# Two-layer graph network on one Trainium2 core: attention slots taken in pairs, scores in quarter tiles, and part of the norm work moved to ScalarE and GpSimd

## The chip, the core and the metric

The kernel runs on one of the eight cores of a Trainium2 chip. The metric is the device time of one execution in microseconds (us), and lower is better. The engines are named as in the profile: PE is the matrix engine (PEld is its weight loading), DVE the vector engine, ACT the scalar engine, POOL GpSimd, and SP the engine that only issues transfers. Each engine works through its own instructions in order and waits on semaphores for the others.

## What is computed

Eight graphs (`B = 8`) of 2048 nodes with 256 features pass through two layers that share one adjacency matrix. All data is float32.

```python
# layer 0: attention with a softmax in each chunk of 256 neighbours, 4 heads of 64
q, k, v = x @ Wq.T + bq, x @ Wk.T + bk, x @ Wv.T + bv
scores = clip(q . k / sqrt(64), -10, 10);  scores = where(mask == 0, -10, scores)
attn = softmax(scores over the 256 nodes of a chunk)
ctx = sum over the 8 chunks of attn @ v
out = layernorm(ctx @ Wo.T + bo + x) * gamma + beta
x = layernorm(x + out)
# layer 1: additive attention, 4 heads of 64
Wh = x @ W;  e = leaky_relu(s_src[i] + s_dst[j], 0.2), masked to -inf
x = layernorm(x + elu(softmax_j(e) @ Wh))
```

## The kernel before

**Slots.** Layer 0 of one graph (a "batch" `b`) is cut into 64 slots (`SLOTS`): four groups `q` of 512 query nodes, two head pairs `hp`, and eight chunks `c` of 256 neighbours. A slot has two units `u`, each of 128 neighbours by 512 queries for two heads. For a unit, `scores` (L390) issues two score matmuls, one per head, with 64 rows of contraction each, into a PSUM buffer of two banks (`ps`). DVE evicts it, clipping it against the mask slab (L401, PSUM to SBUF, `pr`). ACT takes the exponential in place (L413). `product` (L427) multiplies the probabilities of one head of the slot with the values; a column of ones in `vaug` yields the softmax sums. It runs twice per slot, `product(s, 0)` and `product(s, 1)`, into one PSUM bank `psC` each time, and ACT copies it out (L434, `raw`). One slot later `normalize` takes the reciprocal of the sums on DVE (L442) and lets POOL multiply and add into the context (L449, L451).

**Layer 1 of the batch before runs along.** While batch `b` is in layer 0, `Layer1` (`lower`) computes layer 1 of batch `b - 1`. `make` (L743) forms a 128 x 1024 tile `e` on DVE from two SBUF inputs, a row and an edge mask; `use` (L765) multiplies it with the node values in 32 matmul passes. A slot takes two tiles (`STEP = 2`). Two tiles are made ahead, and the pool of `e` has three buffers. `close` divides the sums and applies the ELU when a unit of 16 tiles is done.

**Between the layers.** `Between` handles a group of 512 nodes when its context is complete: output projection (`output`, L543), the two norms, and layer 1's projection (`values`, L585). Its steps are hung into the slots of the next group by tables (`BESIDE`, `BEHIND`, `WIDE_...`, `LATER_...`); the number is the slot within the group of 16. `Norm.stats` uses DVE's batch-norm instructions (L492, L495), and POOL forms the factors (L502, L503). The row additions `bias`, `shift`, `scale`, `again` are on DVE (L527, L531, L560, L563). `Close` ends layer 1: it adds layer 0's result (L830, DVE), norms it and stores it; the table `CLOSING` hangs it into the first slots of a batch.

**Order.** All engines are scheduled by hand: an instruction stands on its engine where the Python line issues it. In a slot with layer 1 along, PE does: scores of the next slot, product 0, two `e` tiles, product 1. DVE does: reciprocal, two evictions, the steps of `Between`, two `e` tiles. Batch 0 has no layer 1 beside it and turns the adjacency into masks instead (`Masks.step`, L251 to L255). Between two batches stands a stretch without slots that projects the next batch's queries, keys and values (L334, L350) and finishes the last group. After batch 7, layer 1 of batch 7 runs alone.

**PSUM.** Eight banks: `psA`, two buffers of two banks, for scores and projections; `psC`, one bank, for products; `psL`, two banks, for layer 1's sums; `psM`, one spare bank.

```python
            if s:
                normalize(s - 1)
            if s + 1 < SLOTS:
                scores(s + 1)
            ...
            product(s, 0)
            if s + 1 < SLOTS:
                for u in range(KT):
                    exps(s + 1, u)
            if lower:
                if b + 1 < B or s < SLOTS - LATE:
                    lower.step()
            ...
                product(s, 1)
```

## Time and profile before

| | |
|---|---|
| median of 3 runs | 3752.97 us (3752.59 to 3754.87) |
| the profiled execution | 3753.24 us, span 3751.5 us |
| granted clock of PE over the span | 0.993 |
| PE, DVE, ACT, POOL busy | 97%, 84%, 53%, 36% |
| HBM traffic | 103 GB/s over the span |

The chain of waits shows when the first score matmul of a batch starts, and cuts the span into stages:

| stage | us |
|---|---|
| start, to the first scores | about 61 |
| batch 0, first scores to last scores | 305 |
| batches 1 to 6, first scores to last scores, each | about 384 |
| stretch between two batches (to the next first scores) | 63 to 68 |
| batch 7, first scores to last scores | about 362 |
| layer 1 of batch 7 alone, and the end | 275.5 |

In the profile a line such as `L401 DVE ... pr<-ps,slab 128x1024 ... x1024 | 1194.3, 1207 | 199.2 <-PE ps L390` gives the line of the kernel, the engine, the tiles out and in, the count, busy time in us, the mean of one in ns, and the idle time of the engine just before. PE's matmuls are pipelined: the ends are modelled, so the distance between starts is the safer measure, and the chain of waits gives it as one duration per run of equal instructions. A float32 matmul shows as two passes on PE, so a score matmul counts twice.

### The profile page before, as it was taken

Reading aid. Unit: us, or ns where it says so; the run is one execution under the profiler, and the core shown is the slowest. Engines: PE = TensorE matmul, PEld = TensorE weight load, DVE = VectorE, ACT = ScalarE, POOL = GpSimd, SP = SyncE. Lnnn points to the kernel's source line nnn. Section 1 sums busy time; section 2 is a strip of 40 time slices with the busy share of each in tenths; the row PEclk is TensorE's granted clock in tenths of the full one; section 3 lists DMA queues with packets and bytes.
Section 4 is the critical chain, followed back from the end, with each engine's and each line's share of the span. In section 5 each row is a group of like instructions: output and inputs, shape, how many; then the busy total and the mean of one; then the engine's idle time right before and its main releaser. Section 6 shows DMA issues by size and latency. Waiting matters only on the chain.

```text
span 3751.5 us, 161119 instructions
## 1 busy us (share of the span) xinstructions
PE 3637.1 (97%) x72844; PEld 2699.4 (72%) x72844; DVE 3139.9 (84%) x4213; ACT 1978.7 (53%) x3571; POOL 1366.8 (36%) x1202
## 2 busy tenths in 40 slices
PE   9999999999999999999999999999999999999787
PEld 5656677776777777776777767777677777776676
DVE  5877489986999689995999959998699977997899
ACT  4666455555555555554555545555455555555322
POOL 1445234333433334333443324433334333334300
PEclk9999999999999999999999999999999999999899
DMA  6653334333333333333433334333433333332354
GB/s 163 152 119 70 79 98 110 103 78 113 105 108 106 86 116 107 105 95 88 132 94 103 98 91 136 109 99 81 113 107 108 105 81 113 116 96 76 103 149 137
DMA packets 672098, 398.56 MB, mean 106 GB/s; under 512 B 427312, under 2 KB 591536, under 8 KB 671408
## 3 DMA queue, kind: packets, MB, share of 16 engines
q1 hardware_dynamic: 621408, 354.55, 36.1%
q10 hardware_dynamic: 50000, 33.70, 2.8%
q8 instruction: 570, 9.34, 1.0%
q14 instruction: 120, 0.98, 0.1%
HBM read 331.22 MB, written 56.89 MB: 103 GB/s over the span
## 4 chain that ended last, share of the span: by engine, by line
PE 84%; DVE 7%; issue 3%; ACT 3%; DMA 1%; SPq 1%; ACTq 0%; POOL 0%; DVEq 0%; POOLq 0%
PE pc L427 25%; PE ps L390 23%; PE pa L765 22%; PE pp L334 5%; PE pw L585 3%; PE po L543 3%; DVE e L743 2%; PE pv L350 2%; DVE pr L401 2%; ACT y L507 1%; ACT pr L413 1%; SPq L284 1%; DMA xp<-in_x_dram 0%; DVE y L563 0%; DVE y L560 0%
## 5 line engine op out<-in xcount | busy, mean ns | idle before, releaser
L401 DVE SCALAR_TENSOR_TENSOR pr<-ps,slab 128x1024 f32<-128x1024 f32 x1024 | 1194.3, 1207 | 199.2 <-PE ps L390 195.2
L427 PEld LDWEIGHTS pc<-vaug,pr 128*64 128x64 f32 x32768 | 1038.6, 138 | 405.4 <-issue 299.0
L743 DVE SCALAR_TENSOR_TENSOR e<-srow,gd,et 128x1024 f32<-128x1024 f32 x1024 | 1278.1, 1292 | 14.9 <-DMA srow<-rowD 8.2
L427 PE MATMUL pc<-vaug,pr 128*64 128x65 f32 x32768 | 1153.4, 224 | 15.7 <-ACT pr L413 9.6
L765 PE MATMUL pa<-waug,e 128*64 128x65 f32 x32768 | 1068.9, 224 | 47.9 <-DVE e L743 43.3
L765 PEld LDWEIGHTS pa<-waug,e 128*64 128x64 f32 x32768 | 1015.5, 139 | 65.7 <-DVE e L743 55.9
L413 ACT ACTIVATE pr<-pr 128x1024 f32<-128x1024 f32 x1024 | 1040.3, 1055 | 40.1 <-DVE pr L401 31.1
L390 PE MATMUL ps<-qT,kT 64*128 64x512 f32 x4096 | 1023.8, 616 | 3.9 <-DVE pr L401 3.2
L434 ACT COPY raw<-pc 128x260 f32<-128x260 f32 x1024 | 380.4, 372 | 1194.1 <-PE pc L427 1175.1
L449 POOL TENSOR_TENSOR part<-raw,rd 128x512 f32<-128x512 f32 x448 | 468.0, 1045 | 1375.7 <-DVE rd L442 1361.3
L451 POOL TENSOR_TENSOR acc<-acc,part 128x512 f32<-128x512 f32 x448 | 574.8, 1283 | 35.2
L390 PEld LDWEIGHTS ps<-qT,kT 64*128 64x128 f32 x4096 | 347.0, 185 | 325.7 <-issue 200.8
L442 DVE RECIPROCAL rd<-raw 128x8 f32<-128x8 f32 x512 | 101.4, 198 | 120.4 <-ACT raw L434 119.3
L449 POOL TENSOR_TENSOR acc<-raw,rd 128x512 f32<-128x512 f32 x64 | 66.8, 1043 | 341.4 <-DVE rd L442 341.4
L797 ACT ACTIVATE sums<-sums,dn 128x64 f32<-128x64 f32 x504 | 131.9, 337 | 13.6 <-DVE dn L791 13.6
L502 POOL TENSOR_TENSOR rs_c<-rs_c,nhalf 128x4 f32<-128x4 f32 x32 | 52.7, 1646 | 233.8 <-DVE off_c L501 233.8
L585 PE MATMUL pw<-w_sb,x1T 128*64 128x264 f32 (+1 forms) x856 | 125.4, 392 | 5.7 <-DVE x1T L296 5.7
L334 PE MATMUL pp<-xT,wk_sb 128*128 128x512 f32 x256 | 119.3, 610 | 7.9 <-ACT qT L342 6.6
L543 PE MATMUL po<-wo_sb,qT 128*64 128x256 f32 (+1 forms) x912 | 120.9, 380 | 6.2 <-DVE qT L469 3.4
L334 PE MATMUL pp<-xT,wq_sb 128*128 128x512 f32 x256 | 116.2, 596 | 0.0
L350 PE MATMUL pv<-wv_sb,xT 128*128 128x256 f32 x512 | 115.9, 379 | 0.0
L296 DVE STREAM_TRANSPOSE xT<-xp 128x1024 f32<-128x1024 f32 x28 | 34.8, 1244 | 92.0 <-PE pw L585 77.8
(103 smaller groups left out, 1869.6 us busy)
## 6 DMA issues: line engine op xcount, KB each, us to landing
et<-edgeD SPq DMA_DIRECT2D x512, 256.0 KB, 3.1
slab<-clipD SPq DMA_DIRECT2D x512, 128.0 KB, 3.1
srow<-rowD SPq DMA_DIRECT2D x64, 512.0 KB, 5.1
xg<-in_x_dram SPq DMA_DIRECT2D x32, 512.0 KB, 5.2
x1D<-y ACTq DMA_DIRECT2D x32, 512.0 KB, 3.9
x1g<-x1D SPq DMA_DIRECT2D x32, 512.0 KB, 5.7
out_dram<-o SPq DMA_DIRECT2D x30, 512.0 KB, 3.6
ctxD<-acc ACTq DMA_DIRECT2D x56, 256.0 KB, 2.6
```

The costliest lines, as they stand in the source:

```text
L334: nc.tensor.matmul(pps[c], lhsT=w[:, kc, c * P : (c + 1) * P], rhs=st["xT"][:, kc, :], start=(kc == 0), stop=(kc == KC - 1),)
L390: nc.tensor.matmul(ps[:, k, :], lhsT=kT[rows, hp, t * P : (t + 1) * P], rhs=qT[rows, hp, cols], start=True, stop=True,)
L401: nc.vector.scalar_tensor_tensor(pr, pss[u], -CLIP, slab[:, u, :].unsqueeze(1).to_broadcast([P, 2, CH]), op0=ALU.max, op1=ALU.min,)
L413: nc.scalar.activation(pr, pr, AF.Exp, scale=0.125)
L427: nc.tensor.matmul(pc[z * D : (z + 1) * D, i, :], lhsT=probs[s][u][:, k, i * P + z * D : i * P + (z + 1) * D], rhs=vaug[:, KT * c + u, 2 * ...
L434: nc.scalar.copy(raws[s][:, k], pc)
L449: nc.gpsimd.tensor_mul(part, raw[:, :, :, :D], rd.to_broadcast([P, 2, QT, D]))
L451: nc.gpsimd.tensor_add(accv, accv, part)
L543: nc.tensor.matmul(po[z, k, :], lhsT=qT[:, c, t * P + z.start : t * P + z.stop], rhs=wo_sb[:, c, :], start=(c == 0), stop=(c == KC - 1),)
L585: nc.tensor.matmul(pw[z, k, : F + 2 * H], lhsT=self.x1T[:, c, u * P + z.start : u * P + z.stop], rhs=w1_sb[:, c, :], start=(c == 0), stop= ...
L743: nc.vector.scalar_tensor_tensor(e[:, :w], self.rows[n][:, :w], self.gd[:, h, j : j + 1], self.edge[k // JG][:, j % JG, :w], op0=ALU.max, ...
L765: nc.tensor.matmul(self.pa[i // QT][z * D : (z + 1) * D, i % QT, :], lhsT=e[:, i * P + z * D : i * P + (z + 1) * D], rhs=self.waug[:, j, h ...
```

## The change

- Two slots form a pair, 32 per batch (`PAIRS`; 8 per group, `QP`). `burst(p)` issues the scores of the four units of the next pair one behind the other. Only three PSUM buffers exist for them, so the fourth unit comes after the first unit's eviction. The other three evictions are spread over the pair.
- `unit` computes a unit's scores as four matmuls of 64 x 64 weights ("quarters"), one per head and half of the neighbours, in place of two of 64 x 128.
- PSUM: `psA` becomes three buffers of two banks in rotation, for scores, products, outputs and projections; `psC` and `psM` are gone. `product(s)` does both heads of a slot at once and is copied out in one go.
- The order on PE in a pair: burst of the next pair, two `e` tiles, product of the first slot, two `e` tiles, product of the second slot.
- Norm statistics in the slots move from DVE to ACT (`sums`, `squares`, with an accumulated output) with small POOL steps (`centre`, `factors`). `bias`, `shift`, `scale` of the groups in the slots and `Close.add` of batches 2 to 7 move from DVE to POOL. The stretches between batches and the end keep them on DVE.
- The steps of `Between` stand in new tables by pair, and the second norm of a group ends one group later (`NEXT_...`) or in the stretch between batches (`early`). Buffers: 7 for `pr` (from 4), 2 slabs of double size (from 4), one `y` (from 2).

```diff
+    def unit(s, u):
+        q, hp, c = where[s]
+        t = KT * c + u
         cols = slice(q * CH, (q + 1) * CH)
-        pss = []
-        for u in range(KT):
-            t = KT * c + u
-            ps = two_banks([P, 2, CH], "ps")
+        ps = two_banks([P, 2, CH], "ps")
+        for z in range(2):
             for k in range(2):
                 rows = slice(k * D, (k + 1) * D)
                 nc.tensor.matmul(
-                    ps[:, k, :],
-                    lhsT=kT[rows, hp, t * P : (t + 1) * P],
+                    ps[z * D : (z + 1) * D, k, :],
+                    lhsT=kT[rows, hp, t * P + z * D : t * P + (z + 1) * D],
                     rhs=qT[rows, hp, cols],
...
+    def burst(p):
+        us = units_of(p)
+        pss = [unit(*us[k]) for k in range(3)]
+        evict(*us[0], pss[0])
+        pss.append(unit(*us[3]))
+        return list(zip(us, pss))[1:]
...
+        def sums(self, ks):
+            for k in ks:
+                junk = small.tile([P, F], BF16, tag="junk", name="junk", bufs=1)
+                nc.scalar.activation(
+                    junk, self.src[:, k, :], AF.Copy, accum_out=self.mv[:, k, 0:1]
+                )
+        def centre(self):
+            self.mean = small.tile([P, QT], F32, tag="mean", name="mean_" + self.name)
+            nc.gpsimd.tensor_scalar(self.mean, self.mv[:, :, 0], -1.0 / F, None, ALU.mult)
+        def squares(self, ks):
+            for k in ks:
+                junk = small.tile([P, F], BF16, tag="junk", name="junk", bufs=1)
+                nc.scalar.activation(junk, self.src[:, k, :], AF.Square,
+                    bias=self.mean[:, k : k + 1], accum_out=self.mv[:, k, 1:2])
+        def factors(self):
...
+            nc.gpsimd.tensor_tensor(self.rs, self.rs, nhalf, ALU.pow)
+            nc.gpsimd.tensor_mul(self.off, self.mean, self.rs)
...
+    FIRST_PAIRS = {2: lambda o: o.add((0, 1)), 3: lambda o: o.add((2, 3))}
+    ON_ACT = {2: lambda o: o.a.sums((0, 1)), 3: lambda o: o.a.sums((2, 3)),
+        4: lambda o: o.a.squares((0, 1, 2, 3)), 5: lambda o: o.a.apply(o.y),
+        7: lambda o: o.b2.sums((0, 1, 2, 3))}
+    LATE_ON = {1: lambda o: o.bias(nc.gpsimd),
+        3: lambda o: (o.a.centre(), o.shift(nc.gpsimd)), 4: lambda o: o.a.factors(),
+        5: lambda o: o.scale(nc.gpsimd), 6: lambda o: o.again(), 7: lambda o: o.b2.centre()}
+    LAST_ON_PE = {1: lambda o: o.output((0, 1)), 2: lambda o: o.output((2, 3))}
+    NEXT_FIRST = {2: lambda o: o.load()}
+    NEXT_ON_ACT = {0: lambda o: o.b2.squares((0, 1, 2, 3)), 1: lambda o: o.finish()}
+    NEXT_LATE = {0: lambda o: o.b2.factors(), 3: lambda o: o.turn()}
+    NEXT_LAST = {4: lambda o: o.values((0, 1)), 5: lambda o: o.values((2, 3))}
...
+            if p:
+                normalize(s0 - 1)
+            hook(FIRST_PAIRS, NEXT_FIRST)
+            if more:
+                waiting = burst(p + 1)
+                evict(*waiting[0][0], waiting[0][1])
+                exps(*us[0])
+                exps(*us[1])
+            hook(ON_ACT, NEXT_ON_ACT)
...
+            if along:
+                along.rest(1)
+                along.make()
+            if more:
+                evict(*waiting[1][0], waiting[1][1])
+                exps(*us[2])
+            if along:
+                along.use()
+                along.make()
+                along.use()
+                along.make()
...
+            product(s0)
+            if more:
+                evict(*waiting[2][0], waiting[2][1])
+                exps(*us[3])
+            normalize(s0)
+            if along:
+                along.rest(1)
+                along.use()
+                along.make()
+                along.use()
...
+            hook(LATE_ON, NEXT_LATE)
+            if closing:
+                closing.do(p, "add", "centre", "factors")
...
+            product(s1)
+            hook(LAST_ON_PE, NEXT_LAST)
...
+            table.setdefault(i, []).append((g, "add", nc.gpsimd))
+            table.setdefault(i + 1, []).extend([(g, "sums"), (g, "centre")])
+            table.setdefault(i + 2, []).extend([(g, "squares"), (g, "factors")])
+            table.setdefault(i + 3, []).append((g, "finish"))
...
+    CLOSING = closing_of((0, 1, 3, 5), ((-1, HOME), (0, HOME), (2, HOME_Y), (4, HOME)))
```

In this excerpt the tables are written on fewer lines than in the file. `turn_context` (a DVE transpose, L469) stands in pairs 1 and 6 of a group, ahead of `LATE_ON`.

436 lines of the change are left out of this document (218 added, 218 removed).

## The prediction

> **What bounds the kernel now.** I read the page's busy shares and chain first, then the chain of waits within batch 3, then single groups, then the timeline where DVE and POOL meet.
>
> ```profile
> PE 3637.1 (97%) x72844; PEld 2699.4 (72%) x72844; DVE 3139.9 (84%) x4213; ACT 1978.7 (53%) x3571; POOL 1366.8 (36%) x1202
> PE 84%; DVE 7%; issue 3%; ACT 3%; DMA 1%; SPq 1%; ACTq 0%; POOL 0%; DVEq 0%; POOLq 0%
> ```
>
> PE carries 84% of the chain. The chain of waits inside a batch shows one slot and, in the stretch between batches, a plain projection:
>
> ```profile
> 1947.16 1.92 PE ps L390 x8
> 1949.08 1.08 PE pc L427 x32
> 1950.16 1.87 PE pa L765 x64
> 1952.03 0.93 PE pc L427 x32
> 1952.96 1.92 PE ps L390 x8
> ...
> 1278.91 3.44 PE pp L334 x8
> ```
>
> A slot repeats every 5.80 us and is PE alone, with no wait in it. The projection gives the price of a 512-column pass: 3.44 / 8 = 0.43. A slot's eight score passes run two at a time, so they need 4 x 0.43 = 1.72, yet take 1.92; the products behind them take 1.08, those behind layer 1's take 0.93. A switch from products to scores thus costs 0.20, the switch back 0.15: 0.35 a slot that no arithmetic needs. The waits view of the whole run has PE idle for DVE only 43.3 us before `pa` (L765) and 3.2 us before `ps` (L390), most of it where layer 1 runs alone. What DVE does beside this costs nothing now, since a slot leaves it slack:
>
> ```profile
> L401 DVE SCALAR_TENSOR_TENSOR pr<-ps,slab 128x1024 f32<-128x1024 f32 x1024 | 1194.3, 1207 | 199.2 <-PE ps L390 195.2
> L743 DVE SCALAR_TENSOR_TENSOR e<-srow,gd,et 128x1024 f32<-128x1024 f32 x1024 | 1278.1, 1292 | 14.9 <-DMA srow<-rowD 8.2
> L434 ACT COPY raw<-pc 128x260 f32<-128x260 f32 x1024 | 380.4, 372 | 1194.1 <-PE pc L427 1175.1
> L449 POOL TENSOR_TENSOR part<-raw,rd 128x512 f32<-128x512 f32 x448 | 468.0, 1045 | 1375.7 <-DVE rd L442 1361.3
> L451 POOL TENSOR_TENSOR acc<-acc,part 128x512 f32<-128x512 f32 x448 | 574.8, 1283 | 35.2
> ```
>
> Last, the timeline of DVE and POOL, in the stretch after batch 7 and in a slot:
>
> ```profile
> 3533.67 8.22 DVE L743 SCALAR_TENSOR_TENSOR e<-srow,gd,et 128x1024 f32<-128x1024 f32 x4
> 3535.06 10.93 POOL L690 TENSOR_TENSOR waug<-waug,ed 128x1024 f32<-128x1024 f32 x4
> ...
> 2060.73 2.30 DVE L401 SCALAR_TENSOR_TENSOR pr<-ps,slab 128x1024 f32<-128x1024 f32 x2
> 2060.89 1.04 POOL L449 TENSOR_TENSOR part<-raw,rd 128x512 f32<-128x512 f32 x1
> 2062.01 1.29 POOL L451 TENSOR_TENSOR acc<-acc,part 128x512 f32<-128x512 f32 x1
> ```
>
> Four `e` tiles beside POOL's products take 8.22, where two in a slot take 2.47 (at 2058.22): 2.06 against 1.24 each. POOL's own go from a median of 1.92 to 2.73. Their times add up, as if they took turns. Evictions (one input in PSUM) lose nothing: 2.30 for two under a POOL product. So each `e` tile (two SBUF inputs) that meets a POOL instruction waits up to its rest. Today POOL's 2.33 us of a slot lie under the two evictions, 2.36.
>
> **The change, part by part.** The sum is made against the profiled execution, 3753.2 (span 3751.5, about 1.7 around it; 0.3 above the median).
>
> *Switches.* One burst per slot pair instead of two: one round trip of 0.35 less, 224 times in batches 1 to 7: **-78**. The Trainium skill's page "TensorEngine Tiling (Array Packing)", Key Properties, says that changing the tiling mode drains the engine; quarters are again another mode than the products' 128 x 64, so by it one trip per burst stays, as taken here.
>
> *Quarters.* Not in this trace. Passes: two row tiles together (0.43 a pair of passes) and two column tiles together (32 pairs of passes in 1.87) both run side by side, so I take four side by side, with 0.43 per step. A 64-column weight load takes 138 ns (L427), a 128-column one 185 (L390), and the first one after a switch is in the open: 0.047 x 224 = **-10**. Bounds: if the switch disappears, another 0.30 x 224 = -67; if the passes of only two quarters interleave, a burst needs nine steps for eight, +0.43 x 224 = +96. The middle is nearest to the two rows that exist.
>
> *DVE in a plain pair.* From the start T of a burst on PE: reciprocal of the last slot at T+0.65 (its products' copy on ACT is over), first eviction at T+1.18 when unit 0 is done, over at T+2.4; PE wants the fourth unit at T+2.67. Own work of a pair: 4 x 1.18 + 4 x 1.235 + 2 x 0.20 = 10.06; PE needs 11.60 - 0.35 = 11.25. POOL's products for the first slot start behind the fourth `e` tile and end at about T'+2.1 of the next burst, those of the second at T'+4.5; the first `e` tile wants T'+3.6 and waits 0.1 to 0.8. That fits the slack of about 1.1: **0**.
>
> *Steps of `Between`, groups 1 to 3.* Gone from DVE per group: three row additions (1.22 each), the statistics (2 x 4 x (0.41 + 0.17) + 0.67 = 5.3). What stays comes in lumps that all stand between the last `e` tile and the next first eviction, and the fourth unit waits behind them. Additions `add` in pairs 2 and 3 (0.68, slack 0.5): 0.17 each. Pair 3: transpose 1.24, so the next first eviction is 0.4 late; `shift` on POOL (1.92, the 128 x 1024 row L690, to 2 x 1.28) then holds up the next first `e` tile, and the second waits for the second slot's L451 (up to 1.1), so the fourth `use` is 0.95 late: 1.35. Pair 6: context transpose 0.70 and `again` 1.22, 0.25 to 0.9 beyond the slack on top of `e` tiles that the `scale` of pair 5 had delayed: 1.3. `bias` and `scale` fall where `output` or `values` gives PE 1.75 more: 0. Together 3.0 x 21 groups = **+63**. By the rule of the Trainium skill, page "SBUF — State Buffer", Who interferes with whom, a DVE instruction with two SBUF inputs and a reading POOL instruction exclude each other for a whole instruction. The rows' 2.06 agree, and by the rule alone `again` would pay up to a full POOL addition. It speaks against the row additions on POOL.
>
> *Closings, batches 2 to 7.* Four additions (taken as 2 x 1.28) in pairs 0, 1, 3, 5 with no PE work beside them; as for `shift`, each costs what the two `e` tiles wait beyond 1.1: about 0.65, together 2.6 x 6 = **+16**. DVE loses 1.25 + 2.6 each, which was hidden.
>
> *ACT.* 16 activations of 128 x 256 per group (y L507: 0.52 apart) and 32 fewer copies per batch (0.1 saved each): ACT goes from 215 to about 245 us of a batch's 384. Cost bounds for the accumulating form, not in the trace: half to twice the row; at twice, four of them hold the second product's copy 2 us back, still before DVE asks for it: **0**. The changed program has one table load, as before.
>
> *POOL's small steps* (the power, 1.0 to 2.05, L502) delay L449 by some 2.4 us; the second `e` tile then waits 0.85, within the slack: 0.
>
> *Batch 0.* Its chain goes through evictions, mask steps and PE; two slots in flight loosen it. Between 0 and -25; I take one switch less per pair, **-11**.
>
> *Between batches.* The same matmuls; the second norm of the group before joins, a chain through ACT, POOL, a store and a load, beside 50 us of PE work. Bounds -3 to +3 each; **0**. The SP queue gets 256 fewer slab issues and the double ones come a full pair ahead: 0. Layer 1 alone: unchanged, 0.
>
> Sum: -78 - 10 - 11 + 63 + 16 = **-20**, so **3733**.
>
> **The rivals.**
> 1. *DVE becomes the bound (slower).* Own work 10.06 plus the batch's lumps (7 context transposes 4.9, 2 turns 2.5, 6 `add` 4.1, 3 `again` 3.7, 8 closes 8.3: 23.5 / 32 = 0.73) is 10.79 a pair. Before, PE took 11.60 + 0.54 for projections = 12.14. From 1.35 us of waiting for POOL per pair on, the change loses. The upper bound is two full waits (1.1 each) and the row steps, over 2; at 2.0: (12.79 - 12.14) x 224 = +146, less batch 0's 11: 3888. For it: POOL stands idle 64% of the span, but in the new order it is busy whenever DVE reaches the first two `e` tiles. Against it: each POOL instruction ahead also gets a burst's evictions as cover.
> 2. *Quarters run in nine steps:* 3733 + 96 = 3829.
> 3. *Quarters need no switch, and POOL waits halve:* 3733 - 67 - 20 = 3646. For it: product tiles and quarters share the 64-column split.
> 4. *Nothing measurable:* lumps cost 20 us more than counted; the upper edge of the forecast.
>
> **How the numbers follow.** The forecast with its own range 3700 to 3770 has 0.44 (0.32 faster, 0.10 the same, 0.02 slower), rival 1 0.26, rival 2 0.10, rival 3 0.20. A difference of 0.2% (7.5 us) is about what a measurement of this kernel can tell from no change. Faster: 0.32 + 0.20 = 0.52; same 0.10; slower 0.02 + 0.26 + 0.10 = 0.38. The range 3640 to 3850 leaves out the upper half of rival 1 and a little of rival 3, some 0.2.
>
> **What would show it.** In the chain of a batch: `ps x32` of about 7.1 per pair, then `pa x64`, `pc x64` twice, every 11.25; 12.1 or more, through DVE, is rival 1; `ps` near 7.5 is rival 2; no excess over 6.88 is rival 3. The waits view should have `ps` and `pa` waiting for DVE by some 80 us in the slots. The mean of `e` should rise from 1292 to about 1450; a mean over 1700 is rival 1. The evictions should stay at 1207. I am wrong most if DVE is on most of the chain, or if the stretches between batches grow by more than 3 us each.

## The result: 3% slower, and the profile after

The changed kernel takes 3867.53 us (median of 4 runs, 3863.30 to 3871.02) against 3753.22 us of the kernel before on the same chip: ratio 1.030, 95% interval 1.029 to 1.032. The forecast was 3733 us, 20 us faster; it is 114 us slower, outside the range of 3640 to 3850.

The profiled execution took 3871.02 us, its span is 3869.2. The page, busy time and chain by engine:

```profile
PE 3608.6 (93%) x76884; PEld 2625.2 (68%) x76884; DVE 3037.3 (78%) x3397; ACT 2262.8 (58%) x4211; POOL 1868.2 (48%) x1442
PE 53%; DVE 25%; issue 9%; POOL 4%; ACT 4%; DMA 3%; SPq 0%; DVEq 0%; ACTq 0%; POOLq 0%
```

PE carried 84% of the chain and now 53%. PE's busy time even fell (3637.1 before); what is new is waiting. By stage, in us (from the starts of score and product matmuls; a batch's slots run from its first scores to its last products, a stretch from there to the next first scores; batches are counted from 0):

| stage | before | after | difference |
|---|---|---|---|
| start to the first scores | 60.6 | 64.7 | +4.1 |
| slots of batch 0 | 312.7 | 303.0 | -9.7 |
| slots of batches 1 to 6, sum | 2363.7 | 2426.6 | +62.9 |
| slots of batch 7 | 369.3 | 371.6 | +2.3 |
| stretch behind batch 0 | 60.4 | 62.0 | +1.6 |
| stretches behind batches 1 to 6, sum | 316.9 | 361.1 | +44.2 |
| from the last products to the end | 267.8 | 280.2 | +12.4 |

So +118, where the forecast had -20: 138 us are missing from its sum. The slots of batches 1 to 7 hold 74 of them (+65, where the forecast's terms add up to -9), the stretches between batches 46 (it had 0), the start and the end 17 (it had 0), and batch 0 one.

The chain of waits inside batch 4 (start, duration, what), first a plain pair, then pair 2 of a group:

```profile
1913.68 3.59 PE ps L392 x32
1917.27 2.02 PE pa L801 x64
1919.29 1.87 PE pc L438 x64
1921.15 1.87 PE pa L801 x64
1923.02 1.87 PE pc L438 x64
1924.89 3.59 PE ps L392 x32
...
1949.92 2.36 POOL xg L569
...
1952.30 0.70 DVE y L596
...
1953.05 1.09 PE ps L392 x8
```

The plain pair is 1924.89 - 1913.68 = 11.21 us, PE alone, as forecast (11.25; two slots took 11.60). But the burst of pair 2 stops at its third unit: its PSUM pair still holds the output's products, which `add` (L596) may only take when GpSimd has added the bias (L569). GpSimd's timeline shows what the bias stands behind, the slot's two normalizing steps:

```profile
1946.69 1.91 POOL L462 TENSOR_TENSOR part<-raw,rd 128x512 f32<-128x512 f32 x1 [5.99 <-DVE rd L455]
1948.69 1.27 POOL L464 TENSOR_TENSOR acc<-acc,part 128x512 f32<-128x512 f32 x1
```

The bias follows them at 1949.92 without a gap, as in all its 24 places on GpSimd, so it is late by its place in GpSimd's order. (The chain has a mask slab's transfer of 3.44 us just ahead of the bias; the bias does not read that slab.) The groups of instructions, by line, with busy time and mean ns, then the idle time ahead of them:

```profile
L779 DVE SCALAR_TENSOR_TENSOR e<-srow,gd,et 128x1024 f32<-128x1024 f32 x1024 | 1385.0, 1379 | 17.4 <-PE pa L801 13.7
L404 DVE SCALAR_TENSOR_TENSOR pr<-ps,slab 128x1024 f32<-128x1024 f32 x1024 | 1217.5, 1214 | 118.8 <-PE ps L392 90.8
L462 POOL TENSOR_TENSOR part<-raw,rd 128x512 f32<-128x512 f32 x448 | 634.5, 1416 | 992.5 <-DVE rd L455 982.1
L464 POOL TENSOR_TENSOR acc<-acc,part 128x512 f32<-128x512 f32 x448 | 668.8, 1493 | 35.1
L445 ACT COPY raw<-pc 128x520 f32<-128x520 f32 x512 | 297.5, 582 | 66.1 <-PE pc L438 63.0
```

Evictions are as before; `e` went from 1292 to 1379, GpSimd's two steps from 1045 and 1283 to 1416 and 1493. What TensorE waited for over the whole run (us, times, longest):

```profile
PE pa L801 <- DVE e L779: 74.9, 96, 4.0
PE ps L392 <- DVE pr L404: 34.6, 65, 4.6
PE pp L337 <- DVE xT L299: 31.6, 7, 5.7
PE ps L392 <- DVE y L596: 29.4, 23, 1.5
PE pt L488 <- POOL acc L464: 13.3, 7, 7.4
PE po L585 <- DVE qT L482: 11.8, 12, 2.0
...
PE ps L392 <- ACT raw L445: 7.8, 17, 1.1
```

Before, VectorE's `e` was the only large entry, and all of it lies behind batch 7's slots, mostly where layer 1 runs alone:

```profile
PE pa L765 <- DVE e L743: 43.3, 30, 4.2
```

Now 39.5 of the 74.9 for `e` are there too, and the list has six further entries, each for a different operand.

To place them, I took for every pair the distance from its first score matmul to the next pair's, less 11.21 and less the output's (1.73) and layer 1's projections (1.78); means of batches 2 to 6, in us. A step that stands behind a pair's last `e` tile holds up the next burst, so what it costs shows in the next pair's column:

| lost in pair | 0 | 1 | 2 | 3 | 4 | 5 | 6 | 7 | sum |
|---|---|---|---|---|---|---|---|---|---|
| group 0 (closings) | 0 | 0 | 0.44 | 0 | 0.86 | 1.57 | 3.10 | 0 | 6.0 |
| group 1 | 0 | 0.84 | 1.77 | 0 | 0.41 | 0.95 | 1.61 | 1.26 | 6.8 |
| group 2 | 0 | 1.63 | 1.77 | 0 | 0.42 | 0.54 | 0.19 | 1.08 | 5.6 |
| group 3 (pairs 0 to 5) | 0 | 1.66 | 1.75 | 0 | 0.41 | 0.03 | | | 3.8 |

With some 2 us in the last pairs that is 24 us a batch; the forecast had 3 x 3.0 + 2.6 = 11.6. Below, "lost in group n" means sums of this kind.

### The profile page after: what moved, and what is told of

The parts are those of the page before. It is cut to its first block, busy times and chain, and to the rows that moved or that the text cites. A ratio compares the mean times of both kernels' runs of the same rounds, so it can differ in the third digit from the quotient of the medians.

```text
span 3869.2 us, 168899 instructions
## 1 busy us (share of the span) xinstructions
PE 3608.6 (93%) x76884; PEld 2625.2 (68%) x76884; DVE 3037.3 (78%) x3397; ACT 2262.8 (58%) x4211; POOL 1868.2 (48%) x1442
## 4 chain that ended last, share of the span: by engine, by line
PE 53%; DVE 25%; issue 9%; POOL 4%; ACT 4%; DMA 3%; SPq 0%; DVEq 0%; ACTq 0%; POOLq 0%
PE pc L438 15%; PE ps L392 14%; PE pa L801 13%; DVE e L779 10%; DVE pr L404 9%; PE pp L337 4%; PE pw L627 3%; PE pv L353 2%; POOL part L462 2%; POOL xg L569 1%; DMA x1D<-y 1%; PE po L585 1%; ACT y L549 1%; ACT raw L445 1%; DVE y L605 1%
## 5 line engine op out<-in xcount | busy, mean ns | idle before, releaser
L779 DVE SCALAR_TENSOR_TENSOR e<-srow,gd,et 128x1024 f32<-128x1024 f32 x1024 | 1385.0, 1379 | 17.4 <-PE pa L801 13.7
L404 DVE SCALAR_TENSOR_TENSOR pr<-ps,slab 128x1024 f32<-128x1024 f32 x1024 | 1217.5, 1214 | 118.8 <-PE ps L392 90.8
L801 PE MATMUL pa<-waug,e 128*64 128x65 f32 x32768 | 1100.6, 225 | 80.8 <-DVE e L779 74.9
L462 POOL TENSOR_TENSOR part<-raw,rd 128x512 f32<-128x512 f32 x448 | 634.5, 1416 | 992.5 <-DVE rd L455 982.1
L438 PE MATMUL pc<-vaug,pr 128*64 128x65 f32 x32768 | 1048.4, 223 | 6.4 <-issue 6.0
L392 PE MATMUL ps<-qT,kT 64*64 64x512 f32 x8192 | 977.0, 601 | 74.3 <-DVE pr L404 34.6
L464 POOL TENSOR_TENSOR acc<-acc,part 128x512 f32<-128x512 f32 x448 | 668.8, 1493 | 35.1
L392 PEld LDWEIGHTS ps<-qT,kT 64*64 64x64 f32 x8192 | 271.7, 132 | 605.2 <-issue 242.2
L445 ACT COPY raw<-pc 128x520 f32<-128x520 f32 x512 | 297.5, 582 | 66.1 <-PE pc L438 63.0
L462 POOL TENSOR_TENSOR acc<-raw,rd 128x512 f32<-128x512 f32 x64 | 117.3, 1833 | 386.3 <-DVE rd L455 386.3
L596 DVE TENSOR_TENSOR y<-po,xg 128x512 f32<-128x512 f32 (+1 forms) x56 | 43.0, 768 | 155.1 <-POOL xg L569 67.7
L585 PE MATMUL po<-wo_sb,qT 128*64 128x256 f32 (+1 forms) x912 | 124.9, 382 | 12.5 <-DVE qT L482 11.8
L337 PEld LDWEIGHTS pp<-xT,wk_sb 128*128 128x128 f32 x256 | 53.7, 218 | 103.8 <-issue 63.5
```

The source lines that it names most:

```text
L337: nc.tensor.matmul(pps[c], lhsT=w[:, kc, c * P : (c + 1) * P], rhs=st["xT"][:, kc, :], start=(kc == 0), stop=(kc == KC - 1),)
L392: nc.tensor.matmul(ps[z * D : (z + 1) * D, k, :], lhsT=kT[rows, hp, t * P + z * D : t * P + (z + 1) * D], rhs=qT[rows, hp, cols], start=Tr ...
L404: nc.vector.scalar_tensor_tensor(pr, ps, -CLIP, row.unsqueeze(1).to_broadcast([P, 2, CH]), op0=ALU.max, op1=ALU.min,)
L438: nc.tensor.matmul(pc[z * D : (z + 1) * D, k, to], lhsT=probs[s][u][:, k, i * P + z * D : i * P + (z + 1) * D], rhs=vaug[:, KT * c + u, 2 ...
L445: nc.scalar.copy(raws[s].rearrange("p k i d -> p k (i d)"), pc[:, :, : QT * D1])
L462: nc.gpsimd.tensor_mul(part, raw[:, :, :, :D], rd.to_broadcast([P, 2, QT, D]))
```

## The experiments

Each kernel is the changed one with the edit shown; times are medians, to be set against 3867.5, each beside its own runs of the kernel before (3751.3 to 3754.0).

**1. The bias a pair earlier (bias_pair0): 3834.1, 33 us less.**

```diff
     LATE_ON = {
-        1: lambda o: o.bias(nc.gpsimd),
+        0: lambda o: o.bias(nc.gpsimd),
```

> The changed kernel with one edit: GpSimd adds the output bias to the block at the end of slot pair 0 instead of pair 1, the pair before VectorE's add reads it. Theory A, late operands: in pair 2 of each of three groups the add of the products waits for this GpSimd addition (67.7 us in 23 waits), holds its PSUM pair and so the third unit of the burst; the 1.75 us that pair 2 loses goes, 21 times: -37 us, near 3830. Theory B, the two engines block each other wherever the addition stands: the loss moves from pair 2 to pair 1 and the time stays within 10 us of the changed kernel's 3867.

Pair 2 loses 0.0 in all three groups instead of 1.75; pair 1, where the addition now ends, loses 0.2 more in group 1 and as much as before in the others; group 0, which holds the closings, loses 0.9 more. The late operand is shown, and the forecast's 0 for `bias` was wrong: it looked at who runs beside the addition, not at who reads it.

**2. Between batches: a y of its own (own_y, 3856.2), then also an earlier turn (turn_early, 3817.5, 50 us less).** In the changed kernel VectorE waits twice:

```profile
DVE y L596 <- POOL xg L569: 67.7, 23, 3.5
DVE y L596 <- DMA x1D<-y: 65.5, 8, 11.1
```

The first is experiment 1's. The second is the single `y` buffer: the last group's `add` needs it, and the group before frees it only with the store behind its second norm, which the change has pushed into the stretch.

```diff
-            self.y = blocks.tile([P, QT, F], F32, tag="y", name="y", bufs=1)
+            self.y = prp.tile([P, QT, F], F32, tag="pr", name="yl")   # last group only
...                                                                    # and turn_early:
-            order += [steps[1], t1, *rest, q0, steps[2], early[3], steps[3], *rest, k1, l2, steps[4], v1]
-            order += [steps[5], q1, early[4], t2, l3, steps[6], ...
+            order += [steps[1], t1, l2, *rest, q0, steps[2], early[3], steps[3], t2, *rest, k1, steps[4], v1]
+            order += [steps[5], q1, early[4], l3, steps[6], ...
```

> The changed kernel with one edit: between two batches the last group's y has a buffer of its own (one of the seven for probabilities) instead of the only y buffer, which the group before frees with its store. Theory A, the buffer: VectorE's add no longer waits 8.1 us for that store, its chain runs about 8 us earlier, the projections' 4.4 us wait for the transposed x goes and with it the lower clock behind it (8 passes in 5.37 us instead of 3.45): each of the seven stretches falls from about 60 to 54 us, -40 us together, and the end of batch 7 by 2 to 6 more: near 3822. Theory B, the statistics: the group before's second norm is still squared, applied, stored, loaded and turned in the stretch, so its own chain and ScalarE's work end last: the stretches fall by at most 2 us each, near 3853.

> The kernel with a y of its own between batches, and one more edit there: the third x block is loaded before the stored y of the group before is asked back, and VectorE turns it before the scale, again and statistics of the last group instead of behind them. Theory A: with a y of its own a stretch still takes 58.8 us against 52.8 of the kernel before because the projection waits 3.7 us for this turned block, which stands on VectorE behind steps that wait for ScalarE's apply, and its 8 passes then take 5.4 us instead of 3.45 at the lower clock after the idle time; both go: -5.6 us in each of seven stretches, 58.8 to 53 or 54, -37 us against that kernel's 3856: near 3819. Theory B, another operand ends last as soon as this one does not (x1 turned, or the GpSimd factors): -1 us a stretch, near 3849.

The first expectation failed in its size: the stretches fell from about 60 to 58.8, because TensorE still waited 3.7 us for the transposed block, which stood on VectorE behind steps that wait for ScalarE. With that moved they are 53.5 (52.8 before the change); 45 of the 50 us lie in the seven stretches. TensorE around the same wait in the changed kernel, where it is 4.36 us (start, us, what, and in brackets the idle time ahead):

```profile
1785.56 3.60 PE L337 MATMUL pp<-xT,wq_sb 128*128 128x512 f32 x8
1793.52 5.37 PE L337 MATMUL pp<-xT,wk_sb 128*128 128x512 f32 x8 [4.36 <-DVE xT L299]
```

The same eight passes take 3.60 ahead of the wait and 5.37 behind it. The windows of the changed kernel, the whole stretch and those eight passes, then the stretch with the early turn (the column behind POOL's is the granted clock, 1.00 being full speed):

```profile
1763.00:1822.50 59.50, 52.98 (x193) 33.84 (x189) 17.07 (x40) 28.95 (x62) 12.13 (x14) 0.97 0.36 76
1793.40:1799.00 5.60, 5.48 (x10) 2.46 (x11) 0.00 (x0) 0.95 (x3) 0.00 (x0) 0.70 0.29 97
1755.00:1808.60 53.60, 52.31 (x327) 31.46 (x326) 25.51 (x46) 27.06 (x46) 10.20 (x9) 1.00 0.40 102
```

The clock is 0.70 over those passes; with the early turn it is 1.00 over the whole stretch. So this wait of 4.4 us costs another 1.8; in own_y the wait is 3.7 us, and the eight passes behind it take 5.37 as well. The Trainium skill's page "TensorE: Matmul & The Clock Gate", What's actually happening, says that an idle window of about 3.4 us halves the clock and a busy one releases it. These two waits agree: behind both, the same passes take half as long again.

**3. Copies and the context turn in another order (raw_turn_first): 3821.1, 46 us less.**

```diff
             normalize(s0)
             if along:
-                along.rest(1)
                 along.use()
+            if i == 1 and q:
+                turn_context(q - 1, 1)      # was behind the last make and use
+            if along:
                 along.make()
                 along.use()
...
             product(s1)
+            if along:
+                along.rest(1)
```

> The changed kernel with two moves: the second step of layer 1's closing in a pair (four scalings on ScalarE, 1.2 us) is issued behind the copy of the pair's second product instead of in front of it, and VectorE turns the stored context ahead of the pair's last e tile instead of behind it. Theory A, late operands again: the third unit of a burst no longer waits 0.7 us for the copy of the products that hold its PSUM pair (7.8 us of waits in all, more behind them), and the output's wait for the turned context (11.8 us on the tile, 21 on its weights) goes: pair 1's 1.6 us in each of three groups falls under 0.4: -25 to -30 us, near 3840. Theory B, VectorE is full in these pairs anyway: the turn ahead of the e tile hands its 0.7 us to the next burst: within 8 us of 3867.

More than expected. Its waits, under the same names as above:

```profile
PE pa L801 <- DVE e L779: 52.9, 56, 3.2
...
PE ps L392 <- ACT raw L445: 6.1, 14, 1.1
...
PE po L585 <- DVE qT L482: 5.8, 4, 2.0
```

The wait for the turned context halved (from 11.8), that for the copy fell little (from 7.8), and the largest part is the wait for `e` tiles, 22 us less. I read this as a consequence: a late burst makes VectorE's evictions late, and the `e` tiles stand behind them. Pair 1 loses 0.0, 0.5 and 0.8 in groups 1 to 3 instead of 0.8, 1.6 and 1.7; pair 2, still with its late bias, 0.3 to 0.9 more. Before the change products had a PSUM bank of their own; now the third unit of a burst needs the PSUM pair that the last product leaves, and ScalarE copied it out behind four scalings of layer 1. Which of the two moves brought more is not separated by a run. In group 0 the turned context has no move, so the 1.1 us that it gains a batch (6.0 to 4.9) come from the scalings; groups 1 to 3 gain 3.0 together.

**4. The two moves between engines, one at a time and both back (rows_dve, stats_dve, pairs_only).**

```diff
-        1: lambda o: o.bias(nc.gpsimd),              # rows_dve: shift, scale and closings' add alike
+        1: lambda o: o.bias(nc.vector),
...
-        2: lambda o: o.a.sums((0, 1)),               # stats_dve: squares, centre, factors go too
+        2: lambda o: o.a.stats((0, 1)),
```

> The changed kernel with the row additions (bias, shift, scale) of groups 0 to 2 and the closings' additions on VectorE at the same places of the program; statistics stay on ScalarE. Theory A+B, the GpSimd additions cost twice, as late operands and by blocking: pair 2's 1.75 us goes, the closings' waits in group 0 fall from 6.0 us a batch to under 2, the mean of an e tile falls from 1379 ns to about 1300: 9 to 12 us a batch, 7 batches, -60 to -85 us, near 3795. Theory C, VectorE has no room for them: a pair takes 11.21 us on TensorE and holds 10.06 us of VectorE work, so each of the 13 additions of 1.22 us a batch puts 0.1 us or more onto its pair, and where one meets a transpose or a second addition over 1 us: only the wait for the bias goes, near 3835 to 3865.

> The changed kernel with the norm statistics of groups 0 to 2 and of the closings back on VectorE (bn_stats, with its small steps) at the places of the sums; row additions stay on GpSimd. Theory S, ScalarE's statistics (0.60 us each, 16 of them in each group) make its exps and its raw copies late: -20 to -40 us, near 3835. Theory C, VectorE has no room: 1.8 us for each of 10 norms a batch, in pairs that have 1.15 us to spare: 0.6 us or more each, 6 a batch, +45 us, near 3910; the stretch between batches gets shorter by 3 us each (-20) because the second norm no longer waits for squares: near 3890.

> The changed kernel with both the statistics and the row additions of groups and closings back on VectorE: only the pairs, bursts, quarters and PSUM pairs of the change are left. If the two moves act apart, their measured single effects add (statistics back +61, row additions back -49): near 3880, and VectorE is the bound in most pairs with a group step. Rival, VectorE is then over the 11.21 us of a pair in nearly all of them: 3920 or more. Second rival, the order of the pairs is itself the gain and the moves were needless: 3750 or less.

| | statistics on ScalarE | statistics on VectorE |
|---|---|---|
| row additions on GpSimd | 3867.5 (as changed) | 3928.2 |
| row additions on VectorE | 3818.8 | 3865.3 |

The statistics on ScalarE gain 61 or 47 us, the additions on GpSimd lose 49 or 63: together nothing. By experiment 1, 33 of the 49 can be the late bias, for in rows_dve pair 2 loses 0.0 as well. rows_dve came between its two expectations, stats_dve 18 us above the worse of its own; its stretches did not get shorter (60.2), so that part was wrong. pairs_only came 15 us under the sum of the single effects: neither rival showed. The Trainium skill's "Perfetto Trace Analysis", Optimizing Scalar/DVE Operations, warns that moving work from VectorE to GpSimd may not help, since they share a read port. The table agrees for the changed kernel; what the port alone costs no run separates, and in the mended kernel of experiment 7 the order is the other way round.

**5. Quarters back to halves (halves): 3867.2, no difference.**

```diff
-        for z in range(2):
-            for k in range(2):
+        for k in range(2):
...
-                    ps[z * D : (z + 1) * D, k, :],
-                    lhsT=kT[rows, hp, t * P + z * D : t * P + (z + 1) * D],
+                    ps[:, k, :],
+                    lhsT=kT[rows, hp, t * P : (t + 1) * P],
```

> The changed kernel with the score tiles as the kernel before has them, 64 rows by 128 columns, two passes a unit instead of four quarters; all else as changed. The prediction's term: a quarter tile saves 0.047 us of first weight load for each of 224 pairs, so the halves cost 10 us more: near 3877. Its rivals: quarters cost nine steps (then the halves gain up to 100 us, 3770), or they spare the switch between scores and products (then the halves lose 60 us or more, 3930). In the profile the plain pair's 11.21 us decides: 11.25, 10.8 or 11.5.

From its chain of waits:

```profile
1911.06 3.63 PE ps L391 x16
...
1922.31 3.63 PE ps L391 x16
```

A plain pair takes 11.25 with halves and 11.21 with quarters, and the loss per burst over the pure passes stays. The term of 0.047 was right in the pair; in the time it drowns in the waits. Rivals 2 and 3 are both out: a burst takes 3.59, where nine steps of 0.43 alone are 3.87, and a pair without the switch would be some 0.30 shorter. (The prediction's signs for a burst, 7.1, 7.5 and 6.88, count its steps twice; by its own 0.43 for each of eight steps the burst is 3.44, and 3.6 with the switch.)

**6. Row additions in four pieces (rows_split): 3850.4, 17 us less, for another reason than thought.**

```diff
-            by.tensor_add(self.r, self.r, row)
+            for k in range(QT):
+                by.tensor_add(self.r[:, k, :], self.r[:, k, :], bo_sb)   # shift, scale, add alike
```

> The changed kernel with each row addition (bias, shift, scale, closing) done in four pieces of 128x256 instead of one instruction of 128x1024; engines and places as changed. Theory B, a GpSimd instruction holds up VectorE's next two-input instruction until it ends: four pieces of about 0.6 us let e tiles in between, the e mean falls from 1379 to about 1340 ns and the closings' 6.0 us a batch to about 4: -15 to -35 us, near 3843. Rival: the time that GpSimd works is the same, so e tiles wait as long in sum, and four starts cost more: within 8 us of 3867, or slower by up to 10.

Its groups:

```profile
L781 DVE SCALAR_TENSOR_TENSOR e<-srow,gd,et 128x1024 f32<-128x1024 f32 x1024 | 1392.1, 1386 | 16.3 <-PE pa L803 13.2 <-DMA srow<-rowD 2.9 <-PE ps L392 0.3
L870 POOL TENSOR_TENSOR h<-h,x1g 128x256 f32<-128x256 f32 x96 | 98.6, 1057 | 0.0
```

The size was within the expectation by luck: the `e` mean rose to 1386 instead of falling, and four pieces of 1057 need longer than the one of 2432. The profiled execution is 27 us under the changed kernel's: the slots of batches 1 to 6 gave 6 of these, the stretches behind them (where VectorE's own additions were split too) 10, batch 0 with its stretch 7, batch 7, the start and the end 4.

**7. The mends together (mend_pool 3753.2, mend_dve 3784.2, mend_split 3769.1, mend_dve_end 3780.8).** mend_pool is experiments 1, 2 and 3 in one kernel; mend_dve takes additions on VectorE instead of the earlier bias; mend_split adds the pieces; mend_dve_end moves one line behind the last slots:

```diff
-            order = [begin, early[0], step, ctx, early[1], step, ...
+            order = [begin, step, early[0], step, ctx, early[1], ...
```

> The edits that paid one by one, together: bias on GpSimd in pair 0 (-33 us against the changed kernel), y of its own and the early turn between batches (-50), the layer 1 scalings behind the products' copy and the context turned ahead of the last e tile (-46). Theory A, separate late operands: the gains add up, -129 us: near 3738, under the kernel before (3753). Theory B, they took the same slack twice: two thirds of it, near 3780.

> As the kernel with the edits together, but all row additions and the closings' additions on VectorE in the changed kernel's places (bias in pair 1). Alone that took off 49 us, 33 of them the wait for the bias, so 16 more than the bias moved: near 3722 if the gains add up. Rival: with the waits gone VectorE is nearer to being the bound (10.1 us of work in a pair of 11.21, plus 1.22 for each addition), and the additions cost what GpSimd's blocking cost: as the other or slower, 3738 to 3750.

> As the kernel with the edits together (bias on GpSimd in pair 0), with the row additions in four pieces of 128x256, which alone took off 17 us: near 3721 if that was what e tiles wait for behind a long GpSimd instruction; near 3738 if those 17 us came from the last quarter of the bias being done early and from the stretches between batches, which the other edits have already mended.

> As the kernel with all edits and its additions on VectorE, and one move behind the last batch's slots: two steps of layer 1 instead of one go ahead of the last context's transposes, which in the changed kernel wait 7.4 us for GpSimd to end its normalizing. Theory: TensorE has work in that wait, -4 to -7 us against the kernel without the move. Rival: layer 1's steps there wait for VectorE's e tiles, which GpSimd holds up, so the wait only changes its name: within 2 us.

mend_pool stands level with the kernel before: ratio 1.000 (0.999 to 1.001). Of 129 us that the single edits took off, 114 remain together. The stretches kept theirs (53.3); the slots of batches 1 to 6 gained 52, where bias and order alone had 27 + 37. mend_dve and mend_split came out slower than both of their expectations. mend_dve turns experiment 4 round: once the operands come in time, the additions on VectorE (the bias in pair 1) are 31 us slower than those on GpSimd. mend_split is 16 us slower than mend_pool: its slots of batches 1 to 6 take 18 more, its stretches behind them 7 less. mend_dve loses 6.6 us in pair 4 of group 0 (mend_pool 1.1). ScalarE's timeline there (pair 4 starts at 1373.4):

```profile
1368.10 2.08 ACT L549 ACTIVATE x1g<-h,off_c,rs_c 128x256 f32<-128x256 f32 x4 [1.31 <-POOL off_c L545]
1370.09 0.49 ACT L532 ACTIVATE junk<-h,mean_c 128x256 bf16<-128x256 f32 x1
1370.48 0.19 ACT L532 ACTIVATION_READ_ACCUMULATOR junk<-h,mean_c 128x1 f32 x1
...
1372.48 1.04 ACT L427 ACTIVATE pr<-pr 128x1024 f32<-128x1024 f32 x1
1373.43 0.57 ACT L445 COPY raw<-pc 128x520 f32<-128x520 f32 x1
```

One closing's apply and the next one's squares stand ahead of the third exp; the copies of both products come late, then VectorE's reciprocal, the closing's addition behind it, and the evictions. The wait for GpSimd behind batch 7 was not worth its move (0.2 us in that stage): it only changes its name.

**8. More order (order_mended 3762.9, order_spread 3770.0, groups_mended 3747.6).** order_mended puts the second norm's factors ahead of the bias, the applies behind the first product's copy, the first context turn a pair later, and keeps layer 1's VectorE steps at their old place; order_spread spreads the closings; groups_mended keeps only what shortened groups 1 to 3.

```diff
             product(s0)
+            hook({}, NEXT_MID)                 # finish of the second norm
...
-            if i == QP // 2 + 2:
+            if i == QP // 2 + 3:
                 turn_context(q, 0)
...                                              # order_spread
-    CLOSING = closing_of((0, 1, 3, 5), ((-1, HOME), (0, HOME), (2, HOME_Y), (4, HOME)))
+    CLOSING = closing_of((0, 2, 4, 6), ((-1, HOME), (1, HOME), (3, HOME_Y), (5, HOME)))
```

> As mend_pool (bias in pair 0 on GpSimd, y of its own, early turn, scalings behind the copy, early context turn), with moves of order alone: the second norm's factors ahead of the bias on GpSimd, the applies of the second norm and of the closings behind the first product's copy on ScalarE instead of ahead of the third exp, layer 1's VectorE steps back at their old place, the first half's context turned a pair later (away from again), and two steps of layer 1 ahead of the last context's transposes. Theory D, in-order queues on ScalarE and GpSimd make the burst's operands late: the 1.2 to 1.7 us of waits in pairs 1, 2 and 7 of each group go, 16 us a batch fall to 8, -45 us: near 3705. Theory C, VectorE has no room left: the waits move to the neighbours, within 12 us of 3753.

> As order_mended with the closings' additions in slot pairs 0, 2, 4 and 6 instead of 0, 1, 3 and 5, so that no pair holds the squares of one block beside the sums or the apply of the next. Theory D: pair 3 and 4 hold less than 11.2 us of ScalarE work, 2 us a batch in six batches: -12 us against order_mended. Theory B, the GpSimd addition holds up e tiles wherever it stands: within 5 us.

> As mend_pool, with those order moves only that shortened groups 1 to 3 in order_mended: factors of the second norm ahead of the bias, its apply behind the first product's copy, the first half's context turned a pair later; the closings and the end of the last batch stay as in mend_pool. Theory D, order: groups 1 to 3 lose 9.4 us a batch instead of 11.4, group 0 stays at 4.6: -2 us in each of seven batches, near 3739, faster than the kernel before. Rival, the sum of waits is set by VectorE and GpSimd: 3748 to 3758.

Theory D fell for the whole: the waits went elsewhere. order_mended is 10 us slower than mend_pool, and order_spread another 7, which neither of its expectations had. TensorE's largest in order_mended:

```profile
PE pa L805 <- DVE e L783: 97.6, 104, 4.0
```

The `e` mean is 1451 there. groups_mended is the best version: ratio 0.9989 (0.9980 to 0.9998), 5 us under the kernel before, less than the 0.2% that I had called measurable; its rival's 3748 to 3758 fits, theory D's 3739 does not.

**9. Why `e` grows (no_norm 3696.2, no_close 3736.2; both leave work out).** First the changed kernel, where VectorE's timeline meets GpSimd's:

```profile
1438.92 3.40 DVE L779 SCALAR_TENSOR_TENSOR e<-srow,gd,et 128x1024 f32<-128x1024 f32 x1
```

```profile
1438.38 2.87 POOL L867 TENSOR_TENSOR h<-h,x1g 128x1024 f32<-128x1024 f32 x1
1441.20 2.03 POOL L462 TENSOR_TENSOR part<-raw,rd 128x512 f32<-128x512 f32 x1
```

The `e` tile ends at 1442.32, 1.07 us after the addition that began ahead of it; the GpSimd multiplication behind it then takes 2.03 instead of 1.05. I set each `e` tile's record against GpSimd's records. Tiles without a GpSimd instruction beside them take 1.27 to 1.28 us on average in each of these kernels; the others make the difference:

| | before | after | mend_pool | groups_mended |
|---|---|---|---|---|
| `e` tiles of 1024 beside a GpSimd instruction | 230 | 478 | 566 | 554 |
| their mean, us | 1.36 | 1.50 | 1.52 | 1.59 |
| `e` tiles over 1.6 us | 5 | 124 | 171 | 195 |

> As mend_pool, but GpSimd normalizes and keeps only the first of each eight products of a head pair; the multiplications and additions of the other seven, 896 GpSimd instructions of 1.0 to 1.6 us, are left out. Theory B, what holds the slots is VectorE's e tiles waiting for these GpSimd instructions: the e mean falls from 1410 to about 1250 ns, the 12 us a batch of waits in batches 1 to 6 nearly go, -70 to -90 us: near 3672. Theory C, VectorE's own 10 us a pair and ScalarE's order hold it: e tiles get shorter, the waits stay: -20 us or less, near 3740.

> As mend_pool, with the closings of batches 0 to 5 (during batches 2 to 7) cut down to the load, one small ScalarE instruction and the store; their additions on GpSimd, sums, squares, factors and applies on ScalarE are left out. If the closings cost what the slots of batches 2 to 6 lose over those of batch 1 (396.7 against 391.1) the time falls by 5.6 us in each of 5 batches and about 4 in batch 7, -32 us: near 3721. The prediction had 2.6 us a batch for them: -16, near 3737.

```diff
-        nc.gpsimd.tensor_mul(part, raw[:, :, :, :D], rd.to_broadcast([P, 2, QT, D]))
-        if c:
-            nc.gpsimd.tensor_add(accv, accv, part)
+        if c == 0:
+            nc.gpsimd.tensor_mul(accv, raw[:, :, :, :D], rd.to_broadcast([P, 2, QT, D]))
```

```diff
-            table.setdefault(i, []).append((g, "add", nc.gpsimd))      # no_close
-            table.setdefault(i + 1, []).extend([(g, "sums"), (g, "centre")])
-            table.setdefault(i + 2, []).extend([(g, "squares"), (g, "factors")])
-            table.setdefault(i + 3, []).append((g, "finish"))
+            table.setdefault(i + 3, []).append((g, "pass"))
```

Without GpSimd's normalizing the time falls by 57 us, between the two expectations, though the `e` mean hardly moves (1410 to 1375). The profiled executions are 60 us apart: 37 of them are in the slots of batches 1 to 6 and 10 in the end, where the wait of 7.5 us for GpSimd's last normalizing is gone. Groups of no_norm:

```profile
L778 DVE SCALAR_TENSOR_TENSOR e<-srow,gd,et 128x1024 f32<-128x1024 f32 x1024 | 1379.1, 1375 | 7.9 <-PE pa L800 5.8 <-DMA srow<-rowD 1.9
L572 POOL TENSOR_TENSOR xg<-xg,beta_sb 128x1024 f32<-128x1024 f32 x24 | 78.2, 3260 | 0.0
L866 POOL TENSOR_TENSOR h<-h,x1g 128x1024 f32<-128x1024 f32 x24 | 69.0, 2875 | 0.0
```

The row additions that stay now fall beside `e` tiles: 49 tiles take over 2.6 us, and the additions stretch to 2.9 and 3.3. The two engines do hold each other up, but the mean of `e` is no measure of the time; I take it that a held tile costs only where no slack is left, which no run shows tile by tile. no_close takes off 17 us: the closings' price in the mended kernel, 16 in the forecast; the 32 that the slots' lengths had suggested did not come.

## Why the prediction was wrong, step by step

The gains were right; what failed are terms that the sum had at 0. They are `bias` (33 us by its own run), "ACT" with the order of the context turn (46), "Between batches" (46 in the stretches; two edits took off 50) and the end (12). In each of them an operand reaches TensorE late: shown by an edit for the first three, and at the end for the wait of 7.4 us for GpSimd alone.

- **Switches and quarters: right.** 11.21 against 11.25. A batch of 32 pairs saves 32 x 0.39 = 12.5 us; over seven that is 87, the forecast's 78 + 10. One trip of about 0.3 stays in a burst, with halves and with quarters.
- **DVE in a plain pair: right.** No wait in it; evictions 1214 (forecast 1207).
- **Steps of `Between`: one named term was right, one did not show, and the largest stood at 0.** The steps of pair 3 (forecast 1.35) would show in pair 4, which loses 0.41; in batch 1's group 0, where no group's step stands, it loses 0.44 too. The additions of pairs 2 and 3 (0.17 each) cost nothing. The steps of pair 6 (forecast 1.3) show in pair 7: 1.26 in group 1 and 1.08 in group 2. In group 1 of batch 3, the context's transpose and `again` stand ahead of the first eviction, and the fourth unit waits for it, as forecast:

```profile
1549.28 0.70 DVE L482 STREAM_TRANSPOSE qT<-ctx 128x512 f32<-128x512 f32 x1
1549.91 1.43 DVE L605 TENSOR_TENSOR y<-y,xg 128x1024 f32<-128x1024 f32 x1
...
1551.38 2.30 DVE L404 SCALAR_TENSOR_TENSOR pr<-ps,slab 128x1024 f32<-128x1024 f32 x2
...
1552.60 1.09 PE L392 MATMUL ps<-qT,kT 64*64 64x512 f32 x8 [1.03 <-DVE pr L404]
```

`bias` "0" is 1.75 in pair 2, 33 us in all: a reader behind a moved producer. The forecast had the groups at 9.0 a batch; they lose 16.2. That they lose 10.2 in groups_mended is near 9.0 by luck: 5.4 of it stand in pairs 1 and 2, where the forecast had next to nothing.
- **ACT: 0 was wrong.** The accumulating form costs 0.41 or 0.51 plus 0.19 for reading the accumulator, within the bounds given. The forecast asked only whether that work delays a copy that VectorE reads; but ScalarE's order counts although it is busy for 58% only: the copy of the products now frees a PSUM pair for the next burst. Moved together with the context turn, that was 46 us.
- **Between batches: the step that failed most plainly.** "0, bounds -3 to +3" is 6.6 to 8.8 a stretch behind batches 1 to 6. I counted the matmuls as the same and the new norm as hidden beside 50 us of PE work. It held the only `y`, put a transpose behind a chain through ScalarE, and let the granted clock fall to 0.70 behind the wait: 50 us, shown by two edits. The change from two `y` buffers to one was in my list of buffers and in none of my sums.
- **Closings: right in size in the mended kernel** (17 by leaving them out, forecast 16). In the changed kernel group 0 loses 6.0 a batch, against 1.5 in batch 1 without closings: 4.5 a batch or 27 in six, where the forecast had 2.6 a batch or 16; no run leaves them out there. **Batch 0: right** (-9.7, forecast -11). **POOL's small steps:** no run tests them alone.
- **Layer 1 alone and the end: 0 was wrong**, +12.4. TensorE waits 7.4 there for GpSimd's last normalizing; without GpSimd's normalizing (no_norm) that wait is gone and the end is 10 us shorter. The rest is not settled. Nor are the 4.1 of the start, which now holds two more mask steps.
- **The rivals.** Rival 1 gave nearly the time (3888) by a mechanism that the runs do not support: not each plain pair is bound by VectorE, a few pairs of each group wait. That the time came near its figure is luck. Its sign, `e` over 1700, did not show; of the rise that the forecast had (1292 to about 1450) about half came (1379). Scores and `e` products wait for VectorE by 99 us ahead of the end, where the forecast had some 80. The forecast's other alarm, stretches that grow by more than 3 us, is what came. Rival 4 (nothing measurable) is out as well.

Undoing the late operands together took off 114 us. mend_pool still stands 20 us over the forecast: 11 of these are in the start and the end (2.8 and 8.0 over the kernel before), the others are waits of the pairs that no single edit removed.

## What to carry to other kernels

When a step moves to another engine or another time, list its readers and its buffer's next owner before its cost: the three largest losses here (33, 50 and 46 us, singly) were operands that came late, not work that found no room. A buffer taken away (two `y` to one, a PSUM bank of its own to a shared rotation) turns the order of the engine that frees it into part of the critical path. Moving VectorE's two-input work to GpSimd is not free while VectorE's other two-input work runs beside it. In the changed kernel it cost 49 to 63 us, much of that by lateness, and ate what ScalarE had gained; with the operands in time it was 31 us better than leaving it on VectorE. So compare the two places again after the order is mended.

## What the hardware showed that I had not expected

- An idle time of 4.36 us on TensorE was followed by eight passes at a granted clock of 0.70, which took 5.37 us instead of 3.60.
- A 128 x 1024 float32 addition takes 2.35 us on GpSimd even in batch 7's last pairs, where no `e` tile runs; on VectorE it takes 1.2.
- ScalarE's accumulated output shows as a second instruction of 0.19 us behind each activation.
- A GpSimd addition that started 0.54 us ahead of an `e` tile seems to have held it: the tile ended 1.07 us after the addition, and the next GpSimd instruction 0.91 after the tile. They took 3.40 and 2.03 us instead of 1.27 and 1.05.
